# q and k channels in another order on the partitions, so that the q stores' outermost dimension is 16 instead of 8

## The chip, the cores and the metric

The kernel runs on one core of a Trainium2 chip. The metric is the time of one execution on the device, in microseconds. Before the change the median of three runs is 3014.15 us (3013.44 to 3031.3).

## The reference, cut to what matters

The network has four layers on x of shape (4, 256, 64, 64), each of the form x + layer(groupnorm(x)). Layers 1 to 3 are 3x3 convolutions and are not touched. Layer 0 is axial attention over the columns, with 16 groups of 32 channels: 8 for q, 8 for k, 16 for v.

```
qkv = einsum('nci,oc->noi', xp, w_qkv)            # 512 output channels
qkv = bn(qkv, ...)                                # statistics over everything
q, k, v = qkv.reshape(N, 16, 32, W)[:, :, :8], [:, :, 8:16], [:, :, 16:]
qe = einsum('ngci,cij->ngij', q, q_emb)
ke = einsum('ngci,cij->ngij', k, k_emb)
qk = einsum('ngki,ngkj->ngij', qe, ke)
sim = bn(concat(qk, qe, ke)) -> summed over the three -> softmax
out = einsum(sim, v) and einsum(sim, v_emb) -> bn -> sum
```

Any order of the 128 q rows and 128 k rows of the projection will do, as long as everything that reads them uses the same order.

## The kernel before, in words

**Stage A, projections (lines 163 to 355).** For each of the four images b, `normalised(b)` loads x in four tiles of 1 MB (`xa`, L186, two halves for each of two channel blocks; six buffers) and takes the statistics of the group norm with `bn_stats` on DVE (L195). Eight chunks k follow: DVE normalises 512 columns (L270), PE multiplies with the weights for q and k (L278, tile `po`) and for v (L293), ACT copies q and k into `qs` (L281) and v into `vs` (L298), DVE takes statistics from `po` (L285), which frees its PSUM bank. At k == 4 `normalised(b + 1)` is put in, and so its `bn_stats` stand in DVE's order among the chunks. ACT stores v to DRAM (`vt_d`, L307) after every second chunk. Between chunks DVE also prepares the weights of layer 1.

When an image's eight chunks are done, the SP queue stores q and k (L322 and L323): two tiles (t = 0 is q, t = 1 is k) by eight column classes l, 16 stores of 256 KB each, with 128 runs of 2 KB. `q_d[b]` has the shape [8 pairs of groups a, 8 classes l, 2 (q, k), 2 parities r, 8 channels c, 512]. A partition of `qs` is (a, r, c), so the store's DRAM side walks a (8, with a step of 512 KiB) outside and (r, c) (16, with a step of 2 KiB) inside.

**Stage B, first pass (lines 383 to 661).** `projections(j)` loads q and k of four groups back (`qb`, L425). `scaled` applies the batch norm's scale and shift (L435), which `spread_scales` (L357 to L374) brings from one row per channel to where it is needed: it multiplies each row's scale with a mask that says which group the row belongs to (`msk`, L366), and adds up the rows of one channel number by a matmul with 0/1 matrices (`M_TKC`, `M_KTRC`, L368). Then come the position terms on PE (L470), the transposes on DVE (L477), and the products (L489). The weights of layer 3 are loaded once (`wr`, L503, on SP after the q stores) and turned into the layer's kernel by an exponential on ACT (L511) and DVE work (L512 to L515).

**Stage C** (from line 664) reads `q_d` again (L724) and does the softmax; the three convolution layers follow.

What sets the order: a scheduler orders each engine's instructions from the program's order and the buffers, and each engine and each DMA queue then goes through its own list in order. On the SP queue the stores L322 of an image stand ahead of the second-half x loads L186 of the image after next. The last image's stores stand ahead of `qb` and `wr`.

Of the kernel before, what the change touches and what calls it, by code (L numbers as in the profile page):

```python
# [17 lines left out]
P = 128  # L18
B = 4
C = 256  # L20
# [3 lines left out]
G = 16  # L24
GP = 8
# [13 lines left out]

@with_exitstack  # L40
def network(ctx: ExitStack, tc, x, wqkv, relm, relt, relw, relv, counts, masks, vecs, rowv, ab, w1, l2w1, l2w2, l3w, mats, out):

# [6 lines left out]
    def scratch(name, shape):  # L51
        return dram.tile(shape, F32, name=name, tag=name)

    q_d = [scratch(f"q_d{b}", [GP, 8, 2, 2, 8, 512]) for b in range(B)]
# [108 lines left out]
    with ExitStack() as ph:  # L163
# [61 lines left out]
        def weights_1(i, name):  # L225
            w = kp.tile([P, 3, C], F32, name=f"{name}_{i}", tag="w", bufs=2)
            nc.sync.dma_start(out=w, in_=w1[i])
            return w
# [35 lines left out]
        for b in range(B):  # L264
            xs, gm, rs = ready
            qs = [qp.tile([P, 8, 8, 64], F32, name=f"qs{t}_{b}", tag="qs") for t in range(2)]
            for k in range(NB):
                xg = gp_.tile([P, 2, 512], F32, name=f"xg_{b}_{k}", tag="xg")
                for t in range(2):
                    nc.vector.tensor_scalar(  # L270
                        xg[:, t, :], xs[t][k // 4][:, bass.ts(k % 4, 512)], gm[:, t : t + 1], rs[:, t : t + 1],
                        ALU.subtract, ALU.mult,
                    )
                for o in range(2):
                    ps = psp.tile([P, 8, 64], F32, name=f"po_{b}_{k}_{o}", tag="po", bufs=3)
                    psf = ps.rearrange("p h w -> p (h w)")
                    for t in range(2):
                        nc.tensor.matmul(  # L278
                            psf, lhsT=wt[:, t, bass.ts(o, P)], rhs=xg[:, t, :], start=(t == 0), stop=(t == 1)
                        )  # L280
                    nc.scalar.copy(  # L281
                        qs[o][:, :, :, bass.ts(k, 8)].rearrange("p l a h -> p h a l"),
                        ps.rearrange("p h (a l) -> p h a l", l=8),
                    )
                    nc.vector.bn_stats(st1[:, o, b * NB + k, :], psf)  # L285
                if k % 2 == 0:
                    vs = vp.tile([P, C, 8], F32, name=f"vs_{b}_{k}", tag="vs")
                for half in range(2):
                    pv = psp.tile([P, 2, C], F32, name=f"pv_{b}_{k}_{half}", tag="pv")
                    for j in range(2):  # L290
                        pix = bass.ts(2 * half + j, P)
                        for t in range(2):
                            nc.tensor.matmul(  # L293
                                pv[:, j, :], lhsT=xg[:, t, pix], rhs=wt[:, t, C : 2 * C],
                                start=(t == 0), stop=(t == 1),
                            )
                    c = 4 * (k % 2) + 2 * half
                    nc.scalar.copy(vs[:, :, c : c + 2], pv.rearrange("p j c -> p c j"))  # L298
                    sq = jp.tile([P, 2, C], F32, name=f"vq_{b}_{k}_{half}", tag="vq")
                    nc.scalar.activation(sq, pv, AF.Square)  # L300
                    squares.append((b, 2 * k + half, sq))
                    if len(squares) > 4:
                        for _ in range(4):
                            add_squares()
                if k % 2 == 1:
                    for r in range(2):
                        nc.scalar.dma_start(  # L307
                            out=vt_d[b][k // 2, r].rearrange("p a c m -> p a (c m)"),
                            in_=vs.rearrange("p (a r c) m -> p r a (c m)", r=2, c=16)[:, r],
                        )  # L310
                if k == 4 and b + 1 < B:
                    ready = normalised(b + 1)
                if b == 0 and 1 < k:
                    threshold(k - 2)
                if b > 0 and k in (1, 5):
                    ternary(2 * (b - 1) + k // 4)
                if k in (3, 7) and 2 * b + k // 4 - 1 in range(len(pieces)):
                    i = 2 * b + k // 4 - 1
                    pieces_1[i] = weights_1(i, "wb")
            for t in range(2):  # L320
                for l in range(8):
                    nc.sync.dma_start(  # L322
                        out=q_d[b][:, l, t].rearrange("a r c f -> a (r c) f"),  # L323
                        in_=qs[t][:, EIGHT[l]].rearrange("p a h -> p (a h)"),
                    )
        while squares:
# [56 lines left out]
    with ExitStack() as ph:  # L383
# [189 lines left out]
        for b in range(B):  # L573
            for gp in range(GP):
# [3 lines left out]
                q = qs[j]  # L578
# [18 lines left out]
        for r in range(2):  # L597
            nc.scalar.dma_start(
                out=qk_d[B - 1][GP - 1].rearrange("(j r) f -> r j f", r=2)[r],
# [649 lines left out]
    with ExitStack() as ph:  # L1249
# [23 lines left out]
        for i, p_ in enumerate((wp1, wp2)):  # L1273
            k = p_.tile([P, 2, 3, 4, 3, 64], BF16, name=f"e_k{i}", tag="k")
# [225 lines left out]
def _matrices():  # L1500

    p = np.arange(P)
    m = np.zeros((P, M_N, P), np.float32)
    m[:, M_ID] = np.eye(P)
    m[:, M_GRP] = (p[:, None] // 8 == p[None, :] // 8) / 8
    m[:, M_GRPS] = ((p[:, None] % 2 == p[None, :] % 2) & (p[:, None] // 16 == p[None, :] // 16)) / 8
    m[:, M_ALL] = 1 / P
    m[:, M_SHUF] = p[None, :] == 2 * (p[:, None] % 64) + p[:, None] // 64
    m[:, M_ODD] = p[None, :] == 2 * (p[:, None] % 64) + 1
    same = p[:, None] % 8 == p[None, :] % 8  # L1510
    for t in range(2):
        m[:, M_TKC + t] = same & (p[None, :] // 64 == t)
        for r in range(2):
            m[:, M_KTRC + 2 * t + r] = same & (p[None, :] // 16 % 2 == t) & (p[None, :] // 8 % 2 == r)
    return m
# [27 lines left out]
def _layout(i):  # L1543
    i = {k: np.asarray(v) for k, v in i.items()}

    def qkv_order(a):
        a = a.reshape(G, 32, -1)[GROUPS]
        return np.concatenate(
            [a[:, :8].reshape(P, -1), a[:, 8:16].reshape(P, -1), a[:, 16:].reshape(C, -1)]
        )  # L1550

    def columns(a, k):
        return a.reshape(k, P).T

    def shuffled(a):
        return a.reshape(2, P).T.reshape(2, P).T

    bn3 = [i[f"L0_conv_bn3_{k}"].reshape(G, 32)[GROUPS].reshape(2, P, 2).transpose(1, 0, 2).reshape(P, 4) for k in ("gamma", "beta")]
    vecs = np.concatenate(
        [columns(qkv_order(i[f"L0_conv_bn1_{k}"]), 4) for k in ("gamma", "beta")]  # L1560
        + bn3
        + [shuffled(i["L1_conv_bias"])]
        + [i["L2_conv_g1"][:, None], i["L2_conv_b1"][:, None]]
        + [columns(i["L2_conv_g2"], 2), columns(i["L2_conv_b2"], 2)]
        + [i["L2_conv_g3"][:, None], i["L2_conv_b3"][:, None]]
        + [columns(i["L3_conv_bias"], 2)]
        + [(np.arange(P) % 2 == 0).astype(np.float32)[:, None]],
        axis=1,
    )
    rel = i["L0_conv_rel_emb"]  # L1570
    ab = [i[f"L3_conv_{k}"].reshape(4, 2, 2).transpose(2, 0, 1).reshape(2, 8) for k in ("alphas", "betas")]
    arrays = {
        "x": i["x"].reshape(B, C, HW),
        "wqkv": qkv_order(i["L0_conv_w_qkv"]).T,
        **_embeddings(rel[:16].reshape(2, 8, 127)),
        "relv": rel[16:, ::-1].T,
        "counts": _counts(),
        "masks": np.repeat(np.eye(G, dtype=np.float32), 8, axis=0),
        "vecs": vecs,
        "rowv": np.concatenate(  # L1580
            [i[f"L0_conv_bn2_{k}"].reshape(3, G)[:, GROUPS].ravel() for k in ("gamma", "beta")] + [i["L1_conv_alpha"]]
        ),
        "ab": np.concatenate(ab, axis=1),
        "w1": i["L1_conv_weight"].reshape(2, P, 2, P, 3, 3).transpose(3, 2, 5, 4, 1, 0).reshape(2, P, 3, 3, C)
        .transpose(0, 2, 1, 3, 4).reshape(6, P, 3, C),
        "l2w1": i["L2_conv_w1"].reshape(2, 64, P, 9).transpose(2, 0, 3, 1),
        "l2w2": i["L2_conv_w2"].reshape(2, 64, 64, 2, 9).transpose(0, 2, 3, 4, 1),
        "l3w": i["L3_conv_weight"].reshape(64, 64, 9).transpose(1, 2, 0),
        "mats": _matrices(),
    }  # L1590
    return {k: np.ascontiguousarray(a) for k, a in arrays.items()}


# [15 lines left out]
```

## Time and profile before

| what | before |
|---|---|
| time, median of three | 3014.15 us |
| span of the profiled execution | 3022.4 us |
| TensorE busy | 2603.3 us, 86% |
| VectorE busy | 2066.0 us, 68% |
| ScalarE busy | 1080.7 us, 36% |
| stage A (0 to 304 us): TensorE, DMA | 251.95 us busy, share 0.64, 206 GB/s |
| start of stage B (304 to 345 us): TensorE, DMA | 22.17 us busy, share 0.57, 172 GB/s |
| L322, issue of one q store on SP | 565 / 1453 / 3985 ns (least, median, most), 64 times |

The busy times are those of the whole execution. The engines' shares are means over stages that have different limits, so a change in one stage has to be read from windows of that stage. "SPq" and "ACTq" rows are DMAs being issued by that engine's queue: the time given is that of issuing, not of the transfer. "DMA share" is the mean busy share of 16 DMA engines in the window.

### The profile page before, as it was taken

The numbers are of one execution on the slowest core, as the hardware profiler recorded it, in microseconds if no ns is written. First come the engines' busy times: TensorE is split into PE (matmuls) and PEld (weight loads), VectorE is DVE, ScalarE is ACT, GpSimd is POOL, SyncE is SP. The second block draws the span as 40 slices with busy tenths as digits, with TensorE's granted clock in tenths as the row PEclk, the third lists the DMA queues.
The fourth block names the chain that finished last, engine by engine and source line by source line (L and its number), as shares of the span: only waits on it lengthen the run. The fifth ranks groups of instructions, "written<-read, shape, count | busy, mean of one in ns | idle before, by whom it ended". The sixth has DMA issues, their size and how long they took to land. (4 is left out here: it accounts for less than half of the span.)

```text
span 3022.4 us, 77554 instructions
## 1 busy us (share of the span) xinstructions
PE 2603.3 (86%) x34248; PEld 1601.9 (53%) x34248; DVE 2066.0 (68%) x3555; ACT 1080.7 (36%) x2073; POOL 55.9 (2%) x119
## 2 busy tenths in 40 slices
PE   7779688999999788778763999999996757999998
PEld 4446456777777566666651444444453433444443
DVE  6454698666666455556657897985787759769553
ACT  4345244555555644444421011111368721101100
POOL 0000000000000100000000000000000000000000
PEclk9889799999999889988986999999997988999999
DMA  6656466545554777778746435323245644343201
GB/s 234 221 166 201 134 167 183 137 124 142 142 135 112 212 241 238 246 237 262 248 169 219 140 113 164 112 97 130 92 140 197 225 176 138 99 146 112 91 28 42
DMA packets 246295, 484.65 MB, mean 160 GB/s; under 512 B 28160, under 2 KB 128128, under 8 KB 220096
## 3 DMA queue, kind: packets, MB, share of 16 engines
q1 hardware_dynamic: 189568, 349.19, 34.7%
q10 hardware_dynamic: 53728, 117.46, 14.3%
q0 software_dynamic: 2656, 12.98, 1.2%
q8 instruction: 271, 4.44, 0.6%
q14 instruction: 72, 0.59, 0.1%
HBM read 283.20 MB, written 196.35 MB: 159 GB/s over the span
## 5 line engine op out<-in xcount | busy, mean ns | idle before, releaser
L997 PE MATMUL gc<-gtr,g_u 128*128 128x512 f32 x1152 | 502.3, 598 | 20.6 <-issue 13.0
L997 PE MATMUL dc<-dtr,d_u 128*128 128x512 f32 x1152 | 504.4, 598 | 17.3 <-DVE dtr L983 11.6
L477 DVE STREAM_TRANSPOSE t<-pd 128x1024 f32<-128x1024 f32 x256 | 304.1, 1227 | 112.7 <-PE pd L470 112.7
L997 PEld LDWEIGHTS gc<-gtr,g_u 128*128 128x128 f32 x1152 | 219.0, 191 | 296.1 <-issue 284.3
L997 PEld LDWEIGHTS dc<-dtr,d_u 128*128 128x128 f32 x1152 | 217.9, 191 | 289.7 <-issue 265.7
L470 PE MATMUL pd<-rm,qb 64*32 64x256 f32 x8192 | 286.1, 389 | 59.4 <-DVE t L477 52.9
L1229 PE MATMUL pc<-e_tr,e_k 128*64 128x512 bf16 x2304 | 264.4, 390 | 39.6 <-ACT pc_o L1237 20.9
L489 PEld LDWEIGHTS pq<-t,t 64*64 64x64 f32 x8192 | 258.6, 135 | 71.6 <-issue 45.7
L489 PE MATMUL pq<-t,t 64*64 64x64 f32 x8192 | 278.2, 220 | 16.2 <-issue 13.4
L493 ACT ACTIVATE o<-pq 128x512 f32<-128x512 f32 x256 | 152.3, 595 | 314.5 <-PE pq L489 314.4
L470 PEld LDWEIGHTS pd<-rm,qb 64*32 64x32 f32 x8192 | 156.4, 108 | 144.5 <-DVE t L477 71.3
L1229 PEld LDWEIGHTS <-e_k 128*64 128x64 bf16 x2304 | 151.6, 112 | 151.2 <-issue 49.6
L796 ACT ACTIVATE pt<-pt,sm 128x512 f32<-128x512 f32 x256 | 162.8, 709 | 189.1 <-DVE pt L766 170.8
L766 DVE TENSOR_TENSOR pt<-e_False,si_False 128x1024 f32<-128x1024 f32 x128 | 151.5, 1217 | 39.0 <-PE e_False L756 34.7
L278 PE MATMUL po<-xg,wt 128*128 128x512 f32 x256 | 123.0, 619 | 33.9 <-DVE st L285 32.3
L498 ACT ACTIVATE pq<-pq 128x512 f32<-128x512 f32 x256 | 149.8, 585 | 3.9
L756 PE MATMUL e_False<-qc_False,rw 32*128 32x256 f32 x1024 | 125.0, 467 | 22.4 <-DVE pt L766 13.9
L1015 ACT COPY gc_c<-gc 128x512 f32<-128x512 f32 x32 | 18.6, 581 | 344.1 <-PE gc L997 344.1
L1015 ACT COPY dc_c<-dc 128x512 f32<-128x512 f32 x32 | 18.7, 584 | 329.2 <-PE dc L997 329.2
L834 PE MATMUL pa_False<-pt,vb 128*32 128x64 f32 x4096 | 103.7, 243 | 32.7 <-issue 22.7
L293 PE MATMUL pv<-wt,xg 128*128 128x256 f32 x512 | 121.5, 386 | 0.0
L807 PE MATMUL den_False<-pt,cnt 128*32 128x128 f32 x2048 | 93.8, 300 | 28.7 <-ACT pt L796 17.6
(383 smaller groups left out, 3393.9 us busy)
## 6 DMA issues: line engine op xcount, KB each, us to landing
si_False<-qk_d SPq DMA_DIRECT2D x64, 1024.0 KB
qk_d<-o ACTq DMA_DIRECT2D x124, 512.0 KB
x<-x_d SPq DMA_DIRECT2D x32, 1056.0 KB
a<-at_d SPq DMA_DIRECT2D x256, 128.0 KB
xa<-in_x SPq DMA_DIRECT2D x16, 1024.0 KB
vt_d<-vs ACTq DMA_DIRECT2D x32, 512.0 KB
q_d<-qs SPq DMA_DIRECT2D x64, 256.0 KB
qb<-q_d SPq DMA_DIRECT2D x128, 128.0 KB
```

Source lines behind the costliest of these rows:

```text
L278: nc.tensor.matmul(psf, lhsT=wt[:, t, bass.ts(o, P)], rhs=xg[:, t, :], start=(t == 0), stop=(t == 1))
L293: nc.tensor.matmul(pv[:, j, :], lhsT=xg[:, t, pix], rhs=wt[:, t, C : 2 * C], start=(t == 0), stop=(t == 1),)
L470: nc.tensor.matmul(pds[t][32 * c : 32 * c + 32, m].rearrange("p j k -> p (j k)"), lhsT=q[rows, 2 * (gp % 2) + g, a, 32 * nb : 32 * nb + 32 ...
L477: nc.vector.transpose(ts[t][:, :, 32 * jh : 32 * jh + 32].rearrange("p a j b -> p j a b"), pds[t].rearrange("p m j k -> p j m k"),)
L489: nc.tensor.matmul(ps[rows, m, :], lhsT=ts[1][rows, n // 2, :, n % 2], rhs=ts[0][rows, n // 2, :, n % 2], start=True, stop=True, tile_posi ...
L493: nc.scalar.activation(o[:, :, 8 * k : 8 * k + 8, :], ps.rearrange("p n (a b) -> p a n b", b=2), AF.Copy, accum_out=acc[:, 0, gp, col : co ...
L498: nc.scalar.activation(psf, psf, AF.Square, accum_out=acc[:, 1, gp, col : col + 1])
L756: nc.tensor.matmul(es[x_ // 2][:, x_ % 2, :, :, par], lhsT=rw[rows, 63 - i : 127 - i].rearrange("p j r -> p (j r)"), rhs=q[rows, :, par, k ...
L766: nc.vector.tensor_tensor(dst, e, src, ALU.add)
L796: nc.scalar.activation(s, s, AF.Exp, scale=s2q[:, gp : gp + 1])
L997: nc.tensor.matmul(ms[k], lhsT=u[:, t, dx, k, bass.ts(co, P)], rhs=vs[t][:, k, :, dx : dx + 64], start=(first and dx == 0), stop=(last and ...
L1229: nc.tensor.matmul(m[64 * g : 64 * g + 64], lhsT=parts[:, g, i, k, dx, :], rhs=vs[g][:, k, 8 * (q % 2) : 8 * (q % 2) + 8, dx : dx + 64], s ...
```

## The change

The rows of q and of k on the partitions are put in the order (r, c, a): parity in the pair of groups, channel, pair, where they were (a, r, c). The DRAM layout of `q_d` stays; the store now walks (r, c) outside, 16 steps of 2 KiB, and a inside, 8 steps of 512 KiB. Everything that has to know which row is which follows on the host: the order of the weights' rows and batch norm parameters, the mask of groups, and the 0/1 matrices of `spread_scales`. It is meant to give the stores an outermost dimension of 16. (A blank line is put in at the top, so lines of the changed kernel count one more.)

```
-                        out=q_d[b][:, l, t].rearrange("a r c f -> a (r c) f"),
+                        out=q_d[b][:, l, t].rearrange("a r c f -> (r c) a f"),
                         in_=qs[t][:, EIGHT[l]].rearrange("p a h -> p (a h)"),
...
-    same = p[:, None] % 8 == p[None, :] % 8
+    same = p[:, None] // 8 % 8 == p[None, :] % 8
...
-        return np.concatenate(
-            [a[:, :8].reshape(P, -1), a[:, 8:16].reshape(P, -1), a[:, 16:].reshape(C, -1)]
-        )
+        q, k = (a[:, i : i + 8].reshape(GP, 2, 8, -1).transpose(1, 2, 0, 3).reshape(P, -1) for i in (0, 8))
+        return np.concatenate([q, k, a[:, 16:].reshape(C, -1)])
...
-        "masks": np.repeat(np.eye(G, dtype=np.float32), 8, axis=0),
+        "masks": (2 * (np.arange(P) % 8) + np.arange(P) // 64)[:, None] == np.arange(G)[None, :],
...
-    return {k: np.ascontiguousarray(a) for k, a in arrays.items()}
+    return {k: np.ascontiguousarray(a, dtype=np.float32) for k, a in arrays.items()}
```

## The prediction

> **What bounds the kernel now.** I read the slices of the page first (the digits are tenths of busy time), to see which stage the change lives in.
>
> ```profile
> PE   7779688999999788778763999999996757999998
> ```
>
> A slice is 75.6 us (3022.4/40). The stores that change belong to the first four to five slices, stage A (projections, 0 to 304 us) and the start of stage B (to 345 us). There TensorE shows 7, 7, 7, 9, 6 and not the 9s of stage B: it waits for something. The chain of waits names the convolutions at the end for most of what it can follow and says nothing of these 345 us, so I took the waits of this stretch:
>
> ```profile
> engine line waited for: us in total, times, longest us
> ...
> DVE sm L195 <- DMA xa<-in_x: 46.6, 4, 19.2
> ...
> PE po L278 <- DVE st L285: 32.3, 3, 15.9
> ...
> ACT L511 <- DMA qb<-q_d: 28.6, 1, 28.6
> ...
> DVE ew L512 <- ACT ew L511: 9.7, 1, 9.7
> ...
> DVE sm L412 <- DMA q_d<-qs: 3.8, 1, 3.8
> ```
>
> Three PE waits of 32.3 us hang on DVE, and DVE hangs on the load of x (18.3 and 19.2 us are two of the four). Why are two loads of x late? The order of the SP queue tells:
>
> ```profile
> start us, us, engine line op out<-in xcount [idle before <-releaser]
> 77.48 25.39 SPq L322 DMA_DIRECT2D q_d<-qs  x16
> ...
> 104.24 2.32 SPq L186 DMA_DIRECT2D xa<-in_x  x2
> ...
> 156.99 25.96 SPq L322 DMA_DIRECT2D q_d<-qs  x16
> 183.05 5.07 SPq L186 DMA_DIRECT2D xa<-in_x  x2
> ...
> 236.76 30.59 SPq L322 DMA_DIRECT2D q_d<-qs  x16
> ...
> 298.41 27.31 SPq L322 DMA_DIRECT2D q_d<-qs  x16
> 325.84 3.51 SPq L425 DMA_DIRECT2D qb<-q_d  x3
> 329.39 2.03 SPq L503 DMA_DIRECT2D wr<-in_l3w  x2
> ```
>
> Sixteen stores of 256 KB hold the SP queue for 25 to 31 us, four times, and the x loads of the second half (L186), or the layer 3 weights (L503), stand behind them. Is the burst bound by bytes or by engines? The windows over two bursts, two load stretches and stage B:
>
> ```profile
> core 0: us, PE busy (x) PEld busy (x) DVE busy (x) ACT busy (x) POOL busy (x), PEclk, DMA share, GB/s
> 107.00:115.00 8.00, 0.00 (x0) 0.00 (x0) 0.34 (x1) 4.72 (x7) 0.00 (x0) 0.62 1.00 335
> 158.00:182.00 24.00, 24.00 (x111) 15.34 (x109) 9.88 (x18) 11.33 (x17) 0.00 (x0) 1.00 0.60 179
> 188.00:195.00 7.00, 0.00 (x0) 0.00 (x0) 0.04 (x1) 1.82 (x3) 0.00 (x0) 0.70 0.94 346
> 299.00:325.00 26.00, 18.07 (x125) 14.29 (x131) 11.77 (x48) 3.97 (x8) 0.00 (x0) 0.65 0.59 169
> 345.00:365.00 20.00, 17.37 (x400) 12.39 (x392) 19.26 (x41) 8.12 (x25) 0.00 (x0) 0.84 0.01 4
> ```
>
> In a burst the engines' mean share is 0.59 to 0.60, though the queue is full; the loads reach 0.94 to 1.00 and 335 to 346 GB/s. The queues of the last burst's 26 us:
>
> ```profile
> q1 hardware_dynamic: 1723, 3.33, 41.1%
> q10 hardware_dynamic: 2080, 1.05, 18.0%
> ```
>
> q1 is SP's queue, here q stores alone, and q10 ACT's, here the vt_d stores. If the q stores have half of the 16 engines, these are loaded by 41.1% plus half of q10's 18.0%, which is 50.1%: exactly eight engines, full, while the other eight have the remaining 9%.
>
> **What the Trainium skill says.** "DMA: Bandwidth & Descriptors", section "Why a DMA increments its semaphore by 16 and not by 1": the number of engines of one DMA is the largest up to 16 that divides the slowest dimensions of both sides, and on this path they are the lowest-numbered ones. The destination was 8 x 16 x 512, so 8 engines; it becomes 16 x 8 x 512 with 128 partitions on the other side, so 16. The 50.1% above agrees. The same page, "Issuing engines are not separate DMA queues": ACT's transfers run on the same engines; the trace agrees, since the 1 MB of vt_d stores and the q stores share the full eight. The same page, "Latency and other measured facts", gives row pitches in HBM: 512 KiB cost little (207 against 214 GB/s), larger ones up to half. No stretch of this trace isolates that.
>
> **The change part by part.**
>
> 1. Relabelled rows (weights, masks, the matrix M_TKC and M_KTRC): other numbers in the same tiles. Instruction order, shapes and counts on PE, DVE, ACT and POOL are the same, and each of the 64 stores keeps its place. Cost 0, with nothing to hide.
>
> 2. The 64 stores. Same bytes and same 2 KB runs. The q1 row gives the price: 0.411 x 26 us x 16 engines = 171 engine-us for 3.33 MB, 51.3 engine-us per MB. A burst of 4.19 MB is 215 engine-us, the vt_d pair beside it (issued 3 to 5 us after the start) 0.180 x 26 x 16 = 75. Before: (215 + 37.5)/8 = 31.6 us from first store to last landing. After: (215 + 75)/16 = 18.1 us. Each burst ends 13.5 us earlier. The cost of issue is no floor: the shortest L322 issue takes 565 ns, 16 of them 9.0 us. Unknown: the price per MB when an engine steps 512 KiB between its 2 KB runs (before, it wrote 32 KB in one piece). Lower bound: full load rate, 5.24 MB at 335 GB/s, 15.6 us. Upper bound: the 8-engine time, 31.6 us. I take 18.1, because 16 engines together still write 32 KB side by side.
>
> 3. First burst. DVE becomes idle at 96.4 us and resumes at 114.66 (18.26 us). After: the stores have landed at 77.5 + 18.1 = 95.6, the x load was issued some 2 us before (its buffer is free from 90.9, when L270 for k=3 ends), takes 1 MB at 335 GB/s = 3.1 us, and some 1.8 us to be signalled: about 100.5. From there DVE needs, as before (114.66 to 120.73), 6.1 us to the statistics that free PE's bank, and PE starts 0.7 later: 107.3, against its own previous end at 106.5. The stall of 14.9 us shrinks to about 1. Also, the clock had fallen to 0.50 to 0.62 and the next four L278 and sixteen L293 matmuls took 3.58 + 3.92 us where 1.83 + 3.46 is usual: 2.2 us more. Saving 14.9 - 1 + 2.2 = 16.1.
>
> 4. Second burst, same sum: landed at 175.1, x usable at 180.2, PE at 187.0 against 185.9. Stall 15.85 becomes 1.1, clock penalty (3.57 + 4.72) - (1.83 + 3.46) = 3.0 goes. Saving 17.7.
>
> 5. Third burst: no x load behind it; PE stalled 1.5 us (at 267.1, behind ACT, which waited to issue vt_d). Saving 1.5.
>
> 6. Fourth burst. DVE L412 waited 3.8 us (316.2 to 320.0) for a store of this burst; it would have landed at 298.4 + 21.6 x 18.1/31.6 = 310.8, so the wait goes. DVE L512 waited 9.7 us for the exponential, which waited for the layer 3 weights, issued at 329.4. After: SP is through with the stores at about 314, three qb loads and the weights are issued by 317, and land about 321.5 (eight-engine qb loads of 0.39 MB ahead of them); table load 1.28 and one exponential 0.44 give 323.2. DVE arrives there at 329.2 - 3.8 = 325.4. Hidden by 2 us. PE, idle 10.9 us behind DVE's transposes, comes with it. Saving 3.8 + 9.7 = 13.5; if the weights land 6 us later, 9.5. Stage B's DVE is full next (19.26 of 20 us), so the shift is passed on.
>
> Nothing later depends on the stores' shape: qb and qc loads read the same addresses with the same patterns.
>
> **Sum.** 16.1 + 17.7 + 1.5 + 13.5 = 48.8 us. 3014.15 - 48.8 = 2965.4, rounded to 2966.
>
> **The rivals.**
>
> - A, the forecast, 2966 us, with stores anywhere from 15.6 to about 21 us: 0.76. For it: 50.1% of the engines, and loads at 335 to 346 GB/s, so the eight idle engines can be used.
> - B, part of it: the scattered writes saturate at about 200 GB/s, or qb loads and vt_d stores crowd the x loads. A burst of 5.24 MB at 200 is 26.2 us, 5.4 us earlier than now. Each of the three large waits gives back 5.4, the third 1: 17 us, 2997 us. For it: no store in these windows shows over 181 GB/s. Against: that is what 8 of 16 engines give. Halfway, at 22 us per burst, it is about 2980. Chance 0.12.
> - C, no change, 3014: the stores' rate doubles but another wait ends at the same place. Candidate: DVE's x loads are then held by their buffer. Against: the buffer is free at 90.9 and the load was issued at 104.2. Or the rate per engine halves. Chance 0.07.
> - D, slower: the pitch of 512 KiB within an engine costs more than half the rate; with 40% of it a burst is 215/0.4/16 + 4.7 = 38.3 us, 6.7 us later than now, in four places 27 us: 3041. Against: the eight engines before already wrote at 512 KiB distance from each other at 19.5 GB/s each. Chance 0.05.
>
> **How the numbers follow.** The range runs from 2953 (A with 15.6 us bursts, no remaining stalls and all clock penalties gone: 17.1 + 18.9 + 1.5 + 13.5 = 51, and 10 us for the spread of the conv stages' clock) to 2994, which takes in the better half of B. Faster by over 1% means under 2984: A and some of B, 0.85. Within 1%: the rest of B and C, 0.10. Slower: 0.05.
>
> **What would show it.** Right: L322's issue time falls from a median of 1453 ns to between 600 and 1000; the share of the engines in a burst rises above 0.85; DVE's wait for xa falls from 46.6 to some 17 us; PE's wait on L285 from 32.3 to 2 or 3; L512's and L412's waits vanish; everything from 345 us on is shifted and as long as before. Wrong: bursts of 16 us or less in SP's queue with the same PE waits (C), or bursts as long as now with a share near 1.0 (D), or a stage after 345 us that grew.

## The result, and the profile after

The changed kernel takes 2979.26 us (median of four, 2976.08 to 2981.28); the kernel before, run beside it, took 3015.06 us. The ratio is 0.9868 (95% interval 0.9833 to 0.9903), which on 3015 us is 40 us less, between 29 and 50; the two medians lie 35.8 us apart. A profile shows one execution, and those of the kernel before scatter: its four times here run from 3013 to 3031 us, and the profiled one took 3024.16. The profiled spans are 3022.4 and 2979.5 us: 42.9 us less, to be accounted for here, some of it scatter. The forecast was 2966 us, 48.8 us less.

First, the SP queue, as before in order of time (start, us of issuing, count last):

```profile
78.65 16.74 SPq L323 DMA_DIRECT2D q_d<-qs  x16
95.48 0.71 SPq L228 DMA_DIRECT2D wb<-in_w  x1
96.29 1.04 SPq L187 DMA_DIRECT2D xa<-in_x  x2
...
144.99 17.30 SPq L323 DMA_DIRECT2D q_d<-qs  x16
162.39 1.10 SPq L187 DMA_DIRECT2D xa<-in_x  x2
...
212.28 17.19 SPq L323 DMA_DIRECT2D q_d<-qs  x16
...
272.17 16.58 SPq L323 DMA_DIRECT2D q_d<-qs  x16
288.86 1.90 SPq L426 DMA_DIRECT2D qb<-q_d  x3
290.81 2.25 SPq L504 DMA_DIRECT2D wr<-in_l3w  x2
```

A burst of 16 stores holds the queue for 16.6 to 17.3 us instead of 25.4 to 30.6, and what stands behind it is issued that much sooner. Three of these bursts and the stretch after the first, by windows (from:to, length, PE, PEld, DVE, ACT, POOL busy, granted clock, DMA share, GB/s):

```profile
79.00:95.00 16.00, 16.00 (x71) 10.31 (x70) 6.29 (x13) 9.10 (x13) 0.00 (x0) 1.00 0.93 276
96.00:105.00 9.00, 9.00 (x46) 5.68 (x45) 1.95 (x4) 5.27 (x8) 0.00 (x0) 1.00 1.00 336
145.00:162.00 17.00, 17.00 (x74) 11.06 (x73) 6.41 (x12) 9.62 (x13) 0.00 (x0) 1.00 0.88 263
272.00:289.00 17.00, 14.42 (x78) 11.55 (x76) 7.81 (x31) 4.11 (x9) 0.00 (x0) 0.79 0.91 273
```

The engines' share is 0.88 to 0.93 where it was 0.60. The queues in 273 to 289 us, of which q1 carries the q stores alone as it did in the window that the prediction used (packets, MB, share of 16 engines):

```profile
q1 hardware_dynamic: 1960, 3.59, 72.1%
q10 hardware_dynamic: 2080, 1.05, 24.1%
```

0.721 x 16 us x 16 engines / 3.59 MB is 51.4 engine-us per MB. The prediction had 51.3 from the trace before. So the price of a megabyte didn't change by a measurable amount, and about twice as many engines paid it. (The traces don't say which engine moved a packet; the number of engines is inferred from these shares.)

Then the waits of the first 420 us:

```profile
DVE sm L196 <- DMA xa<-in_x: 20.3, 3, 7.3
...
ACT L512 <- DMA wr<-in_l3w: 14.2, 1, 14.2
...
PE po L279 <- DVE st L286: 7.6, 2, 3.9
```

DVE waits for x for 20.3 us, not 46.6, and PE behind it 7.6, not 32.3. They are less, and not gone: two stalls of PE of 3.7 and 3.9 us are left. The exponential (L512) still waits for the layer 3 weights, but DVE no longer waits for the exponential. In PE's slices the start reads 7, 9, 9, 9, 8 where it read 7, 7, 7, 9, 6:

```profile
PE   7999889899999778888845999999996848999998
```

Where the 42.9 us are, from the four bursts to stage B's first product (the first instruction of L490, L489 before):

| interval | before | after | saved | forecast |
|---|---|---|---|---|
| burst 1 starts to burst 2 starts | 79.51 | 66.34 | 13.2 | 16.1 |
| burst 2 to burst 3 | 79.77 | 67.29 | 12.5 | 17.7 |
| burst 3 to burst 4 | 61.65 | 59.89 | 1.8 | 1.5 |
| burst 4 to the first product | 47.2 | 31.3 | 15.8 | 13.5 |

That is 43.3 us; the first burst started 1.2 us later, which leaves 42.1, and the first product is indeed at 303.5 us where it was at 345.6. What follows it took 2676.8 us before and 2676.0 after.

### The profile page after: what moved, and what is told of

Read it like the earlier page. It is cut to its first block, busy times and chain, and to the rows that moved or that the text cites. A ratio compares the mean times of both kernels' runs of the same rounds, so it can differ in the third digit from the quotient of the medians.

```text
span 2979.5 us, 77554 instructions
## 1 busy us (share of the span) xinstructions
PE 2605.9 (87%) x34248; PEld 1609.6 (54%) x34248; DVE 2066.4 (69%) x3555; ACT 1084.8 (36%) x2073; POOL 55.7 (2%) x119
## 5 line engine op out<-in xcount | busy, mean ns | idle before, releaser
L490 PEld LDWEIGHTS pq<-t,t 64*64 64x64 f32 x8192 | 261.7, 137 | 72.0 <-issue 46.9
L490 PE MATMUL pq<-t,t 64*64 64x64 f32 x8192 | 281.3, 221 | 16.1 <-issue 14.0
L279 PE MATMUL po<-xg,wt 128*128 128x512 f32 x256 | 123.6, 623 | 9.2 <-DVE st L286 7.6
L859 PE MATMUL pe_False<-pt,ve 128*32 128x64 f32 x4096 | 92.1, 245 | 32.6 <-issue 24.5
```

What stands on the lines that cost most here:

```text
L279: nc.tensor.matmul(psf, lhsT=wt[:, t, bass.ts(o, P)], rhs=xg[:, t, :], start=(t == 0), stop=(t == 1))
L490: nc.tensor.matmul(ps[rows, m, :], lhsT=ts[1][rows, n // 2, :, n % 2], rhs=ts[0][rows, n // 2, :, n % 2], start=True, stop=True, tile_posi ...
```

## The experiments

Each ratio is to the kernel before, run beside it on the same chip; its median there was 3026 to 3029 us, so a time that was expected in us is compared by its ratio. Two theories stood at the start. Theory 1: a store has as many engines as its outermost dimension allows, and eight more engines are the whole of it. Theory 2: it is the order of the partitions or of the writes that made a store faster. A second question came with the result: why were the two x loads usable some 3 us later than forecast?

**The new order, with eight engines (e1_split8).** Each store is cut into its two parities, so that c, 8 steps, is outermost. Rows, bytes and 2 KB runs stay.

```
-    out=q_d[b][:, l, t].rearrange("a r c f -> (r c) a f"),
+    for r in range(2):  # two stores of 64 partitions
+        out=q_d[b][:, l, t, r].rearrange("a c f -> c a f"),
```

> The changed kernel (q and k in the new order), but each 256 KB store is issued as two of 128 KB, one for each parity r, so that the outermost dimension of the DRAM side is 8 again: 128 stores, same bytes, same 2 KB runs, same addresses. Theory 1 (the number of engines is what counts): the bursts are as long as before the change, 25 to 31 us on the SP queue, engines' share in a burst 0.6, the wait of DVE for x back at 40 us or more, time about 3015 us (3005 to 3025). Rival theory 2 (the new order of writes, or the order on the partitions, makes the stores fast, whatever the number of engines): bursts of 17 us or little more and 2979 us.

Measured: 3011.51 us, ratio 0.9939 (0.9911 to 0.9966). The burst on SP, and the queue in 79 to 112 us:

```profile
78.82 33.65 SPq L324 DMA_DIRECT2D q_d<-qs  x32
...
114.22 0.84 SPq L187 DMA_DIRECT2D xa<-in_x  x2
```

```profile
q1 hardware_dynamic: 2063, 3.77, 36.0%
q10 hardware_dynamic: 3953, 2.00, 22.8%
q0 software_dynamic: 144, 0.79, 5.9%
```

In the new order, but with 8 outside, the burst is as long as before, even longer. The price is 0.360 x 33 x 16 / 3.77 = 50.4 engine-us per MB. If the stores have eight engines, and ACT's and GpSimd's queues (q10, q0) spread over all sixteen, those eight are loaded by 36.0 + 11.4 + 2.95 = 50.4% of sixteen: full again. Theory 2 falls: the order gives the stores nothing, the engines do. The time isn't the one expected, since the kernel is still some 18 us faster than before. The trace shows why this time is no clean test: with 32 DMAs the scheduler placed DVE's work in another order, with the statistics of x behind more of the chunks:

```profile
128.01 0.59 PE L111 MATMUL pst<-sm,mt 128*128 128x2 f32 x2 [6.87 <-DVE sm L199]
```

DVE waited 11.5 us for x here, and PE stalled only 6.87 us, where it stalled 14.9 before. So the burst's length is a clean result and the time is confounded.

**Eight engines for the last image alone (e3_last8).** The same cut under `if b == B - 1`; images 0 to 2 keep 16 engines.

> The changed kernel, but the stores of the last image alone are in two halves with 8 outside, as in e1_split8; the other three bursts stay at 16. Tells how much of the gain is in the fourth burst. In the two traces the stretch from the fourth burst's start to the first product matmul became 15.8 us shorter. Theory 1: all of this and only this is lost, 2995 us (2988 to 3001), and DVE waits again about 10 us for the exponential of the layer 3 weights. Rival (the gain of the fourth burst is only the earlier start of the stage): 2979 us.

Measured: 2993.24 us, ratio 0.9893 (0.9854 to 0.9932). The last burst and the waits behind it:

```profile
265.93 27.55 SPq L325 DMA_DIRECT2D q_d<-qs  x32
```

```profile
DVE ew L520 <- ACT ew L519: 10.5, 1, 10.5
...
DVE sm L420 <- DMA q_d<-qs: 1.9, 1, 1.9
```

DVE's wait for the exponential is back (9.7 us before, 10.5 here), and from burst 4 to the first product it takes 46.6 us (47.2 before, 31.3 after). The gain of this fourth place hangs on its own burst, as theory 1 has it. The time alone doesn't show that: the ratio is 0.0025 above the changed kernel's, some 7.5 us, where 15.8 were expected, and both intervals are wider than this.

This kernel is the changed one up to the last image, so it also repeats the second site. Its x load let PE wait 0.98 us there, and the changed kernel's 3.91. PE's instructions of the changed kernel, then of e3_last8:

```profile
177.74 3.78 PE L279 MATMUL po<-xg,wt 128*128 128x512 f32 x4 [3.91 <-DVE st L286]
181.31 4.43 PE L294 MATMUL pv<-wt,xg 128*128 128x256 f32 x16
```

```profile
174.07 1.98 PE L279 MATMUL po<-xg,wt 128*128 128x512 f32 x4 [0.98 <-DVE st L286]
175.89 3.62 PE L294 MATMUL pv<-wt,xg 128*128 128x256 f32 x16
```

After the stall of 3.91 us the next matmuls are slow, from start to start 3.57 and 4.27 us against the usual 1.83 and 3.46; after 0.98 us they are not. So the stall of 3.9 us cost 6.5. Stage A ends at 266.6 us here and at 272.8 in the changed kernel.

**Is it the v stores that delay x? (e5_vt_late).** ACT's pair of `vt_d` stores after chunk 3 of images 1 and 2 is issued one chunk later.

> The changed kernel, but for images 1 and 2 the pair of v stores after chunk 3 (1 MB on the ACT queue) is issued one chunk later, so that it does not run beside the x load that DVE waits for. Nothing else moves. Theory A (what is left of the wait for x, 7.0 and 7.3 us, is crowding: the load shares 16 full engines with this pair): the waits fall by about 3 us each (1.05 MB at 336 GB/s), PE's two stalls of 3.7 and 3.9 us to about 1, time 2970 to 2976 us. Theory B (the load is late only because it stands behind the stores in the queue): waits and stalls as in the changed kernel, 2979 us.

Measured: 2983.34 us, ratio 0.9850 (0.9812 to 0.9888).

```profile
DVE sm L196 <- DMA xa<-in_x: 23.9, 4, 7.8
...
PE po L280 <- DVE st L287: 8.1, 2, 4.4
```

No change. The pair that moved turned out to be another one than that beside the x load, so the edit missed its target. The trace of the changed kernel answers instead. Queues in 96 to 105 us, while x was on its way:

```profile
DMA packets 825, 3.02 MB, mean 336 GB/s; under 512 B 78, under 2 KB 185, under 8 KB 578
q1 hardware_dynamic: 717, 2.95, 97.0%
q10 hardware_dynamic: 107, 0.05, 2.0%
```

ACT's queue has 2.0% of the engines, so v stores do not crowd this load. SP's own queue moved 2.95 MB at full rate, and the size of its packets tells what they were. Those of 8 KB are x: 246 of the 256 of both tiles, 2.02 MB. Of the 393 from 2 KB up to 8 KB, 128 of 3 KB are the `wb` load ahead of x (L228, 0.39 MB); the other 265, of 2 KB, are the last 0.52 MB of the stores and a few of `qb`. DVE waited for the first x tile alone: the second was still moving until 106.2 us, and DVE had resumed at 104.56. So what stood ahead of that tile was 0.52 MB of stores and 0.39 MB of `wb`.

**x ahead of the q stores (e6_defer, e10_all_late).** If what stands ahead in SP's queue is the cause, x must come in time when it doesn't stand behind the stores. In e6_defer the eight k stores of images 0 to 2 are put behind the x loads, in e10_all_late all 16. (The matmuls into `po` have line 291 here.)

```
+    owed += [(b, t, l, qs) for t in range(2) for l in range(8)]   # not stored yet
...
     if k == 4 and b + 1 < B:
         ready = normalised(b + 1)
+    if k > 4:
+        pay(6)        # e10_all_late; e6_defer: k != 4, 2 ahead of k == 4, 3 after it
```

> The changed kernel, but for images 0 to 2 the eight k stores of each image are issued after the second-half x loads instead of ahead of them; the eight q stores stay where they are. Theory B (place in the queue): the x load is issued when its buffer is free and lands before DVE asks or within 3 us; PE's stalls of 3.7 and 3.9 us and the clock drop behind them (1.6 and 2.6 us) are gone, time 2966 to 2972 us. Theory A (crowding by the v stores): the wait for x falls only to about 4 us, and the time to 2973 to 2979 us.

> The changed kernel, with all sixteen stores of images 0 to 2 behind the second-half x loads. Theory B: no wait of PE behind the statistics is left in stage A, which ends at 263 to 267 us (272.8 in the changed kernel), time 6 to 9 us under the changed kernel's in the same call. Rival: the stores then run beside the next image's loads and take the gain back, time as the changed kernel's.

Measured: e6_defer 2986.88 us, ratio 0.9871 (0.9824 to 0.9919); e10_all_late 2981.18 us, ratio 0.9850 (0.9824 to 0.9875). PE's waits in e6_defer, then the SP queue of e10_all_late:

```profile
PE po L291 <- DVE st L298: 1.9, 1, 1.9
PE pst L121 <- DVE sm L113: 3.1, 2, 2.8
```

```profile
91.69 0.80 SPq L187 DMA_DIRECT2D xa<-in_x  x2
92.55 22.58 SPq L269 DMA_DIRECT2D q_d<-qs  x16
```

At the first x load PE stalls 1.9 us in e6_defer and not at all in e10_all_late, where the changed kernel and its repeats have 3.1 to 3.7; at the second it stalls in neither. So what stands ahead in the queue accounts for most of the stalls that were left (7.6 us). New ones come elsewhere: 2.8 us in e6_defer, behind the statistics of the group norm (`pst`), and 2.4 us in e10_all_late at 139 us, where a later x load stands behind the deferred stores. Stage A ends at 266.7 and 265.8 us, 6 to 7 us before the changed kernel's 272.8; this alone would prove little, since e3_last8 came to 266.6 with the old order. The times that were expected didn't come: e6_defer is at the changed kernel's ratio, and beside e10_all_late the changed kernel took 2985.01 us, 3.8 us more instead of 6 to 9, which lie within both intervals.

**The changed kernel once more (after_again).**

> The changed kernel once more, beside e10_all_late and the kernel before on the same chip: 0.985 to 0.990 of the kernel before. A second profile of it shows how much of the differences between two profiles in the first pass and in the attention (663.8 against 670.6 us, 579.6 against 570.3 us) is scatter: theory, all of it, since the change touches nothing there; rival, the first pass is truly 7 us longer (again 670 us) and takes part of the gain back.

Measured: 2985.01 us, ratio 0.9864 (0.9841 to 0.9887). What I wanted from it is how much the later stages scatter. Tile rows of the first products, of the kernel before and then the changed kernel:

```profile
L489 PE MATMUL pq<-t,t x8192: 214/218/363, 345.6 to 1009.4; 64*64 64x64 f32 x200
```

```profile
L490 PE MATMUL pq<-t,t x8192: 214/218/365, 303.5 to 974.1; 64*64 64x64 f32 x200
```

The same in after_again:

```profile
L490 PE MATMUL pq<-t,t x8192: 214/218/364, 303.8 to 968.0; 64*64 64x64 f32 x200
```

The start agrees to 0.3 us, while the pass took 670.6 us once and 664.2 the other time, 663.8 in the kernel before. Six microseconds in that pass are scatter, and nothing that the change did.

**The layer 3 weights past the queue, in the kernel before (e7_before_wr).** `wr` is loaded by the GpSimd queue instead of SP's; the stores keep eight engines.

```
-            nc.sync.dma_start(out=wr[64 * h : 64 * h + 64], in_=l3w)
+            nc.gpsimd.dma_start(out=wr[64 * h : 64 * h + 64], in_=l3w)
```

> The kernel before the change, but the layer 3 weights (wr) are loaded on GpSimd's queue, so that they don't stand behind the last burst of stores on SP's. Theory 1 (in the fourth burst the loss is the place of the weights behind the stores, 9.7 us of DVE's time, beside 3.8 us of waiting for a store): from the fourth burst's start to the first product matmul 37 us instead of 47.2, time about 3005 us where the kernel before has 3015. Rival: something else behind the stores (q and k loads for the next step) holds DVE at the same place, no change.

Measured: 3020.93 us, ratio 0.9989 (0.9973 to 1.0005).

```profile
POOL wr L503 <- DMA q_d<-qs: 27.3, 1, 27.3
...
DVE ew L512 <- ACT ew L511: 3.2, 1, 3.2
```

From burst 4 to the first product it takes 38.4 us instead of 47.2, close to what was expected, and DVE's wait for the exponential fell from 9.7 to 3.2 us. The edit got the weights only part of the way: on GpSimd's queue, too, their load first waited 27.3 us for a q store (L503), and it went out 21.2 us after the burst's start instead of 31.0. So the wait at L512 hangs on when the weights can be issued behind the stores; a load that waits for no store was not tried. The time moved by only 3.3 us, between -8.2 and +1.5, where some 10 were expected. The profiled execution, 3011.88 us, was the fastest of twenty; in it what follows the first product took 2675.8 us, as before. Why the median moved less stays open.

**The order alone, with eight engines (e9_before_defer, e11_before_all_late).** The edits of e6_defer and e10_all_late in the kernel before: can one have the gain without the engines?

> The kernel before the change, with 8 outside, but for images 0 to 2 the eight k stores are issued after the second-half x loads, as in e6_defer. The order of DVE's, PE's and ACT's instructions is that of the kernel before. Theory B (the loss at the first two bursts is the x load's place in the queue behind sixteen slow stores): PE's waits behind L285 fall from 32.3 to under 8 us and stage A ends at 270 to 280 us where it ended at 299, time 2990 to 2995 us. Rival theory (the x load is late because the lower eight engines are full, wherever it stands): waits for x stay above 30 us, time over 3005 us.

> The kernel before the change, 8 outside, with all sixteen stores of images 0 to 2 behind the second-half x loads (in e9_before_defer seven q and k loads, which wait for stores, still stood ahead of the first x load, and there the stall stayed at 13.3 us, while at the second x load it fell to 1.9). Theory B (the loss at the first two bursts is the place of the x load behind the stores): no wait of PE behind the statistics over 3 us is left, stage A ends at 265 to 275 us (299.1 in the kernel before), the first product matmul comes at 310 to 320 us (345.6), time about 0.990 of the kernel before; bursts of stores still take 25 us or more. Rival (the eight engines that the stores fill hold up other transfers just as much: ACT's v stores, q and k loads): stage A ends after 283 us, time above 0.994 of the kernel before.

Measured: e9_before_defer 3020.66 us, ratio 0.9971 (0.9958 to 0.9984). PE at the two sites:

```profile
119.93 3.78 PE L290 MATMUL po<-xg,wt 128*128 128x512 f32 x4 [13.27 <-DVE st L297]
...
196.24 1.98 PE L290 MATMUL po<-xg,wt 128*128 128x512 f32 x4 [1.86 <-DVE st L297]
```

At the second site x went out ahead of the k stores, and the stall of 15.9 us is 1.9. At the first, seven `qb` loads that have to wait for stores stood ahead of it, and 13.3 us are left; another 8.3 us came up at `pst`. Stage A ended at 289.5 us, not at the 270 to 280 that were expected. e11_before_all_late took 3013.86 us, ratio 0.9949 (0.9931 to 0.9967). Its waits, and PE where it stalls now:

```profile
ACT qs L293 <- DMA vt_d<-vs: 17.3, 1, 17.3
```

```profile
134.48 0.59 PE L120 MATMUL pst<-sm,mt 128*128 128x2 f32 x2 [12.45 <-DVE sm L112]
...
202.89 0.59 PE L120 MATMUL pst<-sm,mt 128*128 128x2 f32 x2 [5.01 <-DVE sm L112]
```

PE no longer waits for x by way of L297. But the stores, which hold SP's queue for as long as before, now lie beside ACT's `vt_d` stores: ACT stands still for 17.3 us around the issue of a pair of them, and PE gets stalls of 12.45 and 5.01 us elsewhere. With 16 engines and the same order (e10_all_late) ACT stands still for 5.4 us at that place. That is about what the rival expected (stage A after 283 us, above 0.994). The order alone brings 0.5%, the engines with the old order 1.3 to 1.4%.

The stages of all kernels side by side (us from the start; the end of stage A is taken as the start of its last copy to `qs`, L281 before):

| kernel | stage A ends | first product | burst 4 to first product |
|---|---|---|---|
| before | 299.1 | 345.6 | 47.2 |
| changed, twice | 272.8, 271.4 | 303.5, 303.8 | 31.3 (first) |
| e1_split8 | 286.7 | 331.7 | 45.7 |
| e3_last8 | 266.6 | 312.5 | 46.6 |
| e5_vt_late | 272.6 | 303.4 | |
| e6_defer | 266.7 | 297.1 | |
| e10_all_late | 265.8 | 298.7 | |
| e7_before_wr | 296.6 | 334.3 | 38.4 |
| e9_before_defer | 289.5 | 333.7 | |
| e11_before_all_late | 283.0 | 330.2 | |

## Why the prediction was right, and where it was too high

- **Parts 1 and 2, the stores: right in order and price, 1 to 3 us short in length.** Through stage A and the start of stage B every engine's instructions stand in the same order as before. The forecast price was 51.3 engine-us per MB; 51.4 was measured. L323's median issue time is 732 ns (forecast 600 to 1000), the share in a burst is at or above 0.88 (forecast above 0.85). The cost that I couldn't bound, 512 KiB steps inside an engine, is nothing with runs of 2 KB. That goes with the Trainium skill's "DMA: Bandwidth & Descriptors", section "Latency and other measured facts", which has the full rate nearly kept at this pitch, for copies of 16 KiB rows within HBM. The length of a burst was put too low. By the trace's packets the last store of the four bursts ended 20.0, 21.2, 19.5 and 18.9 us after the first issue, where the sum had 18.1. It took sixteen engines as full from the first issue and as finishing together; the first packet moved 1.2 us after it, and in the first burst some engines carried `wb` from 97.2 us on while others stored until 98.7. Rivals B and D fall with the price, and C with the PE waits. B's halfway case (bursts of 22 us, about 2980 us) comes near the measured time, but not by its cause: the stores and what ran beside them moved at 276 GB/s, which is no limit at 200.

- **Part 3, first burst: 13.2 us, not 16.1.** The term that was mis-sized is the landing of x, "100.5". DVE resumed with it at 104.56:

```profile
104.56 0.69 DVE L196 BATCH_NORM_STATS2 sm<-xa 128x6 f32<-128x512 f32 x1 [7.01 <-DMA xa<-in_x]
```

  The forecast was 23.0 us after the burst's start; it was 25.9, so 2.9 too many. Two things add up to this. The last store ended 20.0 us after the burst's start instead of 18.1: 1.9 us. And between the stores and x stood the `wb` load, which I had left out: 0.39 MB, at 335 GB/s 1.2 us. What I had for x itself, 3.1 us for one tile of 1 MB and 1.8 to be signalled, holds: 4.7 us were left for it where these make 4.9. PE's stall was 3.66 us for the forecast "about 1". The clock also fell: the next four L279 took 3.45 us from start to start where 1.83 is usual, 1.6 more. Stall and clock together are 4.3 us against the 2.9 missing; 1.4 us came back somewhere that I did not find.

- **Part 4, second burst: 12.5 us, not 17.7.** Again the landing of x: DVE waited 7.25 us and PE 3.91. No `wb` stood ahead here; the stores alone were late, the last one 21.2 us after the burst's start, 3.1 more than 18.1, and x was usable 4.7 us after it (forecast 5.1). The windows of the last stores and x on their way, first in the changed kernel, then in e3_last8, where DVE waited 4.3 us:

```profile
162.00:171.00 9.00, 9.00 (x46) 5.71 (x45) 1.71 (x4) 5.13 (x8) 0.00 (x0) 1.00 0.94 285
```

```profile
161.00:168.00 7.00, 7.00 (x26) 4.67 (x25) 2.63 (x5) 4.31 (x6) 0.00 (x0) 1.00 1.01 336
```

  SP's queue moved 2.53 MB in the changed kernel, 2.33 in e3_last8, and the rate was 285 against 336 GB/s. Up to here the two run the same instructions, so this 3 us is scatter; the forecast, a wait of 4.4 us, is what e3_last8 shows. It is the exception: in after_again DVE waited 6.93 us here and PE 3.59. The second mis-sized term weighs as much: the clock penalty, which the sum gave back in full. A stall of 3.91 us was still long enough to lose it: (3.57 + 4.27) - (1.83 + 3.46) = 2.5 us. With the stall's excess of 2.8 over the forecast 1.1 that makes 5.3, for the 5.2 us missing. "TensorE: Matmul & The Clock Gate", section "Part 1: The HAM clock gate (the "warmup" mystery)", puts the fall to half the clock after an idle window of about 3.4 us, and says that the window runs freely. The traces agree in part. Stalls of 3.66 and 3.91 us lost the clock, one of 0.98 us did not. But a stall of 1.94 us in e6_defer lost it too (the granted clock was 0.51 from 109.5 to 113 us):

```profile
108.83 3.15 PE L291 MATMUL po<-xg,wt 128*128 128x512 f32 x4 [1.94 <-DVE st L298]
111.78 4.18 PE L306 MATMUL pv<-wt,xg 128*128 128x256 f32 x16
```

  These four L291 took 2.95 us from start to start instead of 1.83, and after a stall of 2.38 us in e10_all_late they took 3.44. One of 1.86 us in e9_before_defer and one of 2.84 us in e6_defer lost nothing. So shorter stalls than 3.4 us can lose the clock, and the length alone doesn't decide.

- **Part 5, third burst: right,** 1.8 for 1.5 us.

- **Part 6, fourth burst: right in the mechanism, 15.8 us for 13.5.** The wait at L413 is 0.2 us, DVE's for the exponential is gone; e3_last8 brings it back by eight engines in this burst alone. The other 2.3 us weren't tested. The windows from burst to first product suggest where they are: the same 276 matmuls took 28.37 us of PE before and 25.25 after, at a granted clock of 0.66 and 0.78.

- **Everything later as long as before: right within scatter.** That 2676.8 and 2676.0 us are so close is luck: the first pass scatters by 6 us, and in after_again what follows the first product took 2681.8.

Together: 16.1 + 17.7 + 1.5 + 13.5 = 48.8 forecast; 13.2 + 12.5 + 1.8 + 15.8 = 43.3, less 1.2 for the later start and with 0.8 later on, 42.9 measured.

## What to carry to other kernels

When the DMA share stands at about half while a queue is full, look at the outermost dimension of what is in it; then price the transfer in engine-us per MB and divide by the engines that it will have. Engine time is not yet the burst's length: add the time to the first packet and the uneven end, here 1 to 3 us on 18. For what stands behind a burst, list everything ahead of it in its queue with its bytes, small loads too: here a later end of the stores and 0.39 MB of `wb` turned 4 us of wait into 7. And if a stall remains, count slow matmuls after it as possible: here stalls from 1.9 us on lost the clock in some places.

## What the runs showed of the hardware

- A store in 2 KB runs with 16 rows outside, whose runs lie 512 KiB apart, costs 51.4 engine-us per MB, and 51.3 with 8 rows outside that are 32 KB in one piece (50.4 with 8 outside and steps of 512 KiB). I had given a loss there 1 in 20, and a partial one more.
- A stall of 3.66 or 3.91 us cost 1.6 or 2.5 us more in slow matmuls; one of 0.98 us cost nothing more. Shorter than 3.4 us is not safe: 1.94 us lost the clock in one place, 2.84 us did not in another. One and the same sequence of instructions ended stage A at 272.8 us and at 266.6 us (e3_last8), where x let DVE wait 3 us less at the second site.
- The end of the second burst and the x load behind it moved at 285 GB/s once and at 336 another time, with the same instructions around them.
- With the stores put off while they have 8 rows outside, ACT stood still for 17.3 us at the issue of its own stores; with 16 outside, for 5.4 us.
